# Layer 2's spectra: two frequency rows in one PSUM tile, copied together, the mirrored operand in its own order

## The chip, the cores and the metric

The kernel runs on one core of a Trainium2 chip. The metric is device time in microseconds of one execution; lower is better. All data are fp32. The engines are named as in the profile: PE (TensorE matmul; PEld is its weight load), DVE (VectorE), ACT (ScalarE), POOL (GpSimd), SP (SyncE, which here issues the DMAs).

## The reference, cut to what matters

Four layers, each adding to a residual `x` of shape (2, 128, 64, 64) what it makes of the group-normalised `x`. The change is in layer 2 alone: a 2-d real Fourier transform of the four quaternion parts (32 channels each), a product with complex weights of its own at each frequency, mixed over input channels by the quaternion rule, and the inverse transform.

```python
xs = jnp.stack([x[:, :q], x[:, q:2 * q], x[:, 2 * q:3 * q], x[:, 3 * q:]])
Xs = jnp.fft.rfft2(xs, s=(64, 64), axes=(-2, -1))
Ws = jnp.stack([kr_w + 1j * ki_w, kr_x + 1j * ki_x, kr_y + 1j * ki_y, kr_z + 1j * ki_z])
C = jnp.einsum('piohw,qbihw->pqbohw', Ws, Xs)
Pw = C[0, 0] - C[1, 1] - C[2, 2] - C[3, 3]
Px = C[0, 1] + C[1, 0] + C[2, 3] - C[3, 2]
Py = C[0, 2] - C[1, 3] + C[2, 0] + C[3, 1]
Pz = C[0, 3] + C[1, 2] - C[2, 1] + C[3, 0]
o = jnp.fft.irfft2(jnp.stack([Pw, Px, Py, Pz]), s=(64, 64), axes=(-2, -1))
```

There are 64 x 33 frequencies. Of the 64 rows over h, row m and row 64 - m (its mirror) come from the same real data.

## The kernel before, in words

Layers 0, 1 and 3 come before and after; layer 2 (`_layer2`) has three parts. First, the input is normalised, transposed and transformed over h into `y`, which stays in SBUF (lines 833 to 891). Last, the result is transformed back over h and added to `X` (from line 1117). Between them stands the part that the change touches: the transform over w, the products and the inverse over w, in eight blocks (`BLOCKS2`) of four frequency rows with their four mirrored rows.

One block `kb` goes like this. For a row m, `transposed` makes two transposes (L912, one per batch element) into a PSUM bank, copied by ACT to `yt` (L918). `transformed` multiplies `yt` with a constant (L925) and leaves in a PSUM bank `pe` (tag `pe`, two buffers of one bank) for each of the 128 channels the spectrum of the row and of its mirror: per batch element 2 images x 34 frequencies x (real, imaginary), 272 numbers in all. `placed` copies this into the operand `e` of the products: for each of the four output parts r, each quaternion part p is taken from channel group r xor p, with a sign. That is 12 copies per row and image of 136 elements per partition: one over 128 partitions with a sign per partition (`signs`), one over 64 and ten over 32. Image 0 is the row, image 1 the mirror, and each image has its own tile `e`, (128, 4 rows, 34, 16). Two rows go together through `rows_in`: `together` takes a step of each row's `placed` in turn, the copies of the first row all on ACT (L948) and those of the second all on DVE (L950).

`products` walks 17 pairs of frequencies (`PAIRS`) for the four rows of an image. Each pair is four products of `e` (32 columns) with the weights (L1008; in the profile each fp32 matmul is two instructions, so eight per group), in four column groups of the PE, whose results land in PSUM banks; DVE transposes them to `z` after each fourth pair (L1017), and L1025 adds and subtracts the parts into `pz`. A row of the mirrored image is stored so that row s of `e` meets row s of the weights, that is, in flipped order (`3 - row`). `turned` transposes `pz` (L1037) and ACT copies it to `pzt` (L1044); `back` transforms over w (L1062) and ACT copies into `y` (L1065).

The order is written out by hand, and each engine keeps it (`_in_order`). For each block, `alongside` runs the 17 groups of the direct products, and then the 17 of the mirrored ones, and after each group takes as many steps of the side generators as `n` says: beside the direct products the first two rows of the next block (`rows_in`, 8 of the steps in `n`) and the last block's `turned` and `back` (6); beside the mirrored ones the next two rows (8) and this block's `turned` (4). What is left of the sides when the products end runs after them. `rows_of_weights` (L823) loads the weights of one half-block on SP's queue, two DMAs of 2112 KB, into one of two buffers (`l2_w`, bufs=2), so a load is issued when the products of the half-block two before have ended. [...]

Of the kernel before, what the change touches and what calls it, by code (L numbers as in the profile page):

```python
# [10 lines left out]
F32 = mybir.dt.float32  # L11
# [5 lines left out]
B, C, H, W = 2, 128, 64, 64  # L17
S = H * W
CH = 512
# [81 lines left out]
def _load_consts(nc, pool, src, n):  # L101
    array, where = _CONSTS[n]
    t = pool.tile([128, array.shape[1]], F32, tag=f"consts{n}", name=f"consts{n}")
    nc.sync.dma_start(t, src)
    return {k: t[:rows, lo:hi] for k, (rows, lo, hi) in where.items()}
# [667 lines left out]
PAIRS = (FW + 1) // 2  # L773
# [29 lines left out]
def _layer2(ctx, tc, X, weights, cst, src, here=None, there=None, beside=None):  # L803


    nc = tc.nc
# [6 lines left out]
    k = _load_consts(nc, one, src, 1)  # L813
# [5 lines left out]
    def rows_of_weights(kb, mirror):  # L819

        ws = wpool.tile([128, 2, 32, NF], F32, tag="w", name="w_ri")
        for n, part in enumerate("ri"):
            nc.sync.dma_start(ws[:, n], weights[kb, mirror, part])  # L823
        return ws
# [5 lines left out]
    with tc.tile_pool(name="l2_a", bufs=3) as ap, tc.tile_pool(  # L830
        name="l2_aps", bufs=4, space=PSUM
# [17 lines left out]
        for b in range(B):  # L849
# [29 lines left out]
            def transformed(i, gt):  # L879
                py = aps.tile([128, CH], F32, tag="py", name="ps_py")  # L880
                for n in range(4):
                    cols = slice(n * 128, (n + 1) * 128)
                    nc.tensor.matmul(py[:, cols], gt[:, cols], k["fwd_h"], start=True, stop=True)
                nc.scalar.copy(
                    y[:, b, 8 * i : 8 * i + 8, :, :].rearrange("p w c f -> p (w c f)"), py
                )
# [11 lines left out]
    with tc.tile_pool(name="l2_e", bufs=4) as ep, tc.tile_pool(  # L898
        name="l2_ps", bufs=2, space=PSUM
    ) as psp, tc.tile_pool(name="l2_pz", bufs=1, space=PSUM) as pzp:  # L900

        def bank(tag="bank"):
            return psp.tile([128, CH], F32, tag=tag, name=f"ps_{tag}")

        def spectra(kb):

            return [(4 * kb + 1 + j) % (FH - 1) for j in range(4)]
# [10 lines left out]
            nc.scalar.copy(yt.rearrange("p b i -> p (b i)"), pt[:, : B * 128])  # L918
            return yt

        def transformed(m, yt):

            pe = bank("pe")
            for b in range(B):
                nc.tensor.matmul(  # L925
                    pe[:, b * 8 * PAIRS : (b + 1) * 8 * PAIRS],
                    yt[:, b, :],
                    k["fwd_w_both" if m else "fwd_w_ends"],
                    start=True,
                    stop=True,  # L930
                )
            return pe[:, : B * 8 * PAIRS].rearrange("p (b s f c) -> p b s f c", b=B, s=2, c=2)

        def placed(kb, m, got, image, e, scalar):

            row = (m - 1) % 4
            s, row = (1, 3 - row) if image else (0, row)

            def copied(r, p, n=1):
                to = slice(32 * p, 32 * p + 32 * n)
                of = slice(32 * (r ^ p), 32 * (r ^ p) + 32 * n)
                sign = signs if n == 4 else float(SIGN2[r][p])
                out = e[to, row, :, 4 * r : 4 * r + 4].rearrange("p f (b c) -> p b f c", c=2)
                sign = sign[to, :] if n == 4 else sign
                if scalar:
                    nc.scalar.mul(out, got[of, :, s], sign)  # L948
                else:
                    nc.vector.tensor_scalar_mul(out, got[of, :, s], sign)  # L950

            copied(0, 0, 4)
            copied(2, 2, 2)
            copied(2, 0)
            copied(2, 1)
            yield
            for r in (1, 3):
                for p in range(4):
                    copied(r, p)
                yield  # L960

        def together(*gens):

            gens = list(gens)
            while gens:
                for g in list(gens):
                    if next(g, gens) is gens:
                        gens.remove(g)
                yield

        def rows_in(kb, rows, places, es):

            yts = [transposed(m) for m in rows]
            yield
            gots = [transformed(m, yt) for m, yt in zip(rows, yts)]
            yield
            yield from copies(kb, rows, gots, places, es)

        def copies(kb, rows, gots, places, es):
            for image in places:  # L980
                if es[image] is None:
                    es[image] = ep.tile([128, 4, 2 * PAIRS, 8 * B], F32, tag="e", name="e")
                yield from together(
                    *(
                        placed(kb, m, got, image, es[image], i % 2 == 0)
                        for i, (m, got) in enumerate(zip(rows, gots))
                    )
                )

        def products(ws, e, pz):  # L990

            z = two.tile([128, PAIRS, 2, 4, 16], F32, name="z", bufs=1)
            zf = z.rearrange("p j n a x -> p (j n a x)")
            for j in range(PAIRS):
                last = j == PAIRS - 1
                if j % 4 == 0:
                    ph = bank() if last else pzp.tile([128, CH], F32, tag=f"z{j}", name="ps_z")  # L1000
                for s in range(4):
                    fw = s * FW + 2 * j
                    if last:
                        w = ws[:, :, :, fw : fw + 1].to_broadcast([128, 2, 32, 2])
                    else:
                        w = ws[:, :, :, fw : fw + 2]
                    out = ph[32 * s : 32 * s + 32, j % 4 * 128 : j % 4 * 128 + 128]
                    nc.tensor.matmul(  # L1008
                        out.rearrange("p (n f o) -> p n f o", n=2, f=2),
                        e[:, s, 2 * j : 2 * j + 2, :].rearrange("p f x -> p (f x)"),  # L1010
                        w.rearrange("p n o f -> p n f o"),
                        start=True,
                        stop=True,
                    )
                if j % 4 == 3 or last:
                    lo, n = j // 4 * CH, (j % 4 + 1) * 128
                    nc.vector.transpose(zf[:, lo : lo + n], ph[:, :n])  # L1017
                yield

            for c in range(2):  # L1020
                parts = [
                    z[:, :, n, 0::3, (c + n) % 2 :: 2]
                    for n in range(2)
                ]
                nc.vector.tensor_tensor(  # L1025
                    pz[:, :, :, c].rearrange("p x (j f) -> p j f x", f=2),
                    *parts,
                    ALU.add if c else ALU.subtract,
                )
            yield  # L1030
# [40 lines left out]
        def chain(*gens):  # L1071
            for g in gens:
                yield from g

        def alongside(main, side, steps):

            done = 0
            for n, _ in enumerate(main):
                while done < steps * (n + 1) / PAIRS:
                    next(side, None)  # L1080
                    done += 1
            for _ in side:
                pass

        pzs = [
            two.tile([128, 4 * B, 2 * PAIRS, 2], F32, name=f"pz{n}", bufs=1) for n in range(2)
        ]
        es = [None, None]
        first = spectra(0)
        for i in (0, 2):  # L1090
            for _ in rows_in(0, first[i : i + 2], (0,), es):
                pass
        before, later = None, []
        for kb in range(BLOCKS2):
            direct, image = [], []
            e, es = es, [None, None]
            nxt = spectra(kb + 1) if kb + 1 < BLOCKS2 else []
            side, n = [], 0
            if nxt:
                side.append(rows_in(kb + 1, nxt[:2], (1, 0), es))  # L1100
                n += 8
            if before:
                side += [turned(pzs[1], before[1]), back(kb - 1, *before)]
                n += 6
            else:
                later = side
                side, n = [rows_in(0, first[i : i + 2], (1,), e) for i in (0, 2)], 10
            alongside(products(rows_of_weights(kb, False), e[0], pzs[0]), chain(*side), n)
            side, n = [turned(pzs[0], direct)], 4
            if nxt:  # L1110
                side = later + [rows_in(kb + 1, nxt[2:], (1, 0), es)] + side
                n += 8 + 8 * len(later)
                later = []
            alongside(products(rows_of_weights(kb, True), e[1], pzs[1]), chain(*side), n)
            before = (direct, image)
        for _ in chain(turned(pzs[1], before[1]), back(BLOCKS2 - 1, *before)):
            pass
# [4 lines left out]
    with tc.tile_pool(name="l2_c", bufs=3) as cp, tc.tile_pool(  # L1122
        name="l2_cps", bufs=4, space=PSUM
# [1338 lines left out]
```

## Time and profile before

| | us |
|---|---|
| three runs | 4132.41, 4122.99, 4132.37 |
| median | 4132.37 |
| the profiled execution | 4122.99 |
| its span on the core | 4121.1 |

| stretch of the span, us | what | PE busy | DVE busy | ACT busy | mean granted PE clock | DMA share |
|---|---|---|---|---|---|---|
| 1918 to 2186 | layer 2, frequency blocks | 234.75 | 182.33 | 152.90 | 0.90 | 0.58 |
| 2186 to 2240 | layer 2 back over h, start of layer 3 | 41.90 | 28.84 | 19.14 | 0.82 | 0.18 |
| 2240 to 4121 | layer 3 | 1853.68 | 1398.69 | 1777.49 | 0.99 | 0.12 |

| line | what, in 1918 to 2186 | count | mean ns |
|---|---|---|---|
| L948 | ACT copy to `e`, 136 elements; with `signs` | 352; 32 | 282; 378 |
| L950 | DVE copy to `e`, 136 elements; with `signs` | 352; 32 | 297; 342 |
| L918 | ACT copy of 256 elements to `yt` | 36 | 373 |
| L1017 | DVE transpose of 512 elements to `z` | 64 | 712 |
| L925 | PE transform over w, 136 columns | 144 | 357 |
| L1008 | PE products, 128 columns | 2176 | 409 |

Matmuls are pipelined: the mean of one is its latency, and how fast they follow one another is read from the start times of the groups in the timeline. The timeline merges neighbouring instructions of one line into one row with a count. "Idle before" names what the engine waited for last.

### The profile page before, as it was taken

What the parts mean: (1) busy time and instruction counts of PE and PEld (TensorE: products, weight loads), DVE (VectorE), ACT (ScalarE), POOL (GpSimd) and SP (SyncE); (2) the same over time, 40 slices, a digit from 0 to 9 for tenths busy, and PEclk for the clock granted to TensorE, in tenths of its full rate; (3) what the DMA queues carried; (4) which work ended last, traced back from release to release, by engine and by line L of the source; (5) the groups of instructions that cost most, each with busy time, mean ns of one, the idle gap of its engine ahead of it and who ended that gap; (6) DMA issues with size and microseconds to landing.
All of it is one profiled execution on the core that took longest, in us unless ns stands there. A gap on an engine that the chain in (4) does not pass through costs nothing. (4 is left out here: it accounts for less than half of the span.)

```text
span 4121.1 us, 83188 instructions
## 1 busy us (share of the span) xinstructions
PE 3944.4 (96%) x35790; PEld 1382.1 (34%) x35790; DVE 3183.8 (77%) x3526; ACT 3228.6 (78%) x3907; POOL 72.2 (2%) x145
## 2 busy tenths in 40 slices
PE   7999999989999998997898999999999999999998
PEld 4522222245222223445665332223222332222222
DVE  4689999747989998986775878767777777766666
ACT  4478888734888884334654899999999999999998
POOL 1001000000000001000000000000000000000000
PEclk9999999999999999998998999999999999999999
DMA  1199970000000000003673211111112011110000
GB/s 49 24 192 180 181 104 2 2 2 2 2 2 2 1 2 13 0 1 132 254 281 104 74 32 34 43 43 32 32 34 67 19 32 32 36 53 6 6 6 4
DMA packets 193133, 217.66 MB, mean 53 GB/s; under 512 B 30441, under 2 KB 154345, under 8 KB 188658
## 3 DMA queue, kind: packets, MB, share of 16 engines
q1 hardware_dynamic: 192754, 212.25, 20.2%
q8 instruction: 282, 4.62, 0.5%
q14 instruction: 97, 0.79, 0.1%
HBM read 178.64 MB, written 98.57 MB: 67 GB/s over the span
## 5 line engine op out<-in xcount | busy, mean ns | idle before, releaser
L2181 ACT ACTIVATE weights<-ps_s 128x1024 f32<-128x1024 f32 x1920 | 1780.6, 1078 | 93.8 <-PE ps_s L2167 93.7
L1379 ACT ACTIVATE weights<-ps_s 128x1024 f32<-128x1024 f32 x1024 | 992.9, 1023 | 169.3 <-PE ps_s L1370 151.1
L2190 PE MATMUL ps_acc<-weights,vt 128*32 128x512 f32 x8192 | 1094.5, 606 | 0.0
L1827 DVE TENSOR_TENSOR sums<-sums,weights 128x2048 f32<-128x2048 f32 x384 | 880.0, 2292 | 43.7 <-ACT weights L1379 7.4
L2167 PE MATMUL ps_s<-q,k 64*128 64x512 f32 x4096 | 838.4, 472 | 6.3 <-DVE exp_i L2123 3.0
L2167 PEld LDWEIGHTS ps_s<-q,k 64*128 64x128 f32 x4096 | 352.7, 184 | 948.4 <-ACT weights L2181 824.7
L1370 PE MATMUL ps_s<-q,k 32*64 32x512 f32 x8192 | 631.5, 614 | 3.7 <-ACT weights L1379 1.5
L1787 PE MATMUL ps_acc<-weights,vt 128*32 128x512 f32 x4096 | 550.0, 605 | 7.2 <-ACT used L1817 3.7
L2139 DVE SCALAR_TENSOR_TENSOR exp_z<-exp_z,exp_m 128x1024 f32<-128x1024 f32 x384 | 469.7, 1223 | 11.2
L2123 DVE TENSOR_SCALAR exp_i<-ps_s 128x1024 int32<-128x1024 f32 x128 | 156.7, 1224 | 254.0 <-PE ps_s L2167 253.1
L1370 PEld LDWEIGHTS ps_s<-q,k 32*64 32x64 f32 x8192 | 162.0, 130 | 435.1 <-PE ps_s L1370 337.9
L2190 PEld LDWEIGHTS ps_acc<-weights,vt 128*32 128x32 f32 x8192 | 161.9, 108 | 304.2 <-issue 303.4
L1787 PEld LDWEIGHTS ps_acc<-weights,vt 128*32 128x32 f32 x4096 | 81.1, 108 | 426.6 <-issue 403.1
L662 DVE SCALAR_TENSOR_TENSOR X<-g,w,X 128x2048 f32<-128x2048 f32 x84 | 197.4, 2351 | 2.6
L1827 DVE TENSOR_TENSOR sums<-weights 128x2048 f32<-128x2048 f32 x64 | 146.6, 2291 | 62.8 <-ACT weights L1379 62.6
L2143 DVE SCALAR_TENSOR_TENSOR weights<-exp_z,exp_i 128x1024 f32<-128x1024 f32 x128 | 156.7, 1224 | 13.9
L1575 PE MATMUL ps_sp<-pad,diag 32*32 32x512 f32 x4608 | 159.8, 600 | 2.3 <-ACT q L1595 1.3
L2139 DVE SCALAR_TENSOR_TENSOR exp_z<-exp_m 128x1024 f32<-128x1024 f32 x128 | 155.9, 1218 | 0.0
L1008 PE MATMUL ps_z<-w_ri,e 128*32 128x128 f32 x2048 | 137.4, 409 | 14.5 <-DVE e L950 12.4
L1575 PEld LDWEIGHTS ps_sp<-pad,diag 32*32 32x32 f32 x4608 | 95.3, 103 | 55.5 <-issue 17.1
L950 DVE TENSOR_SCALAR e<-ps_pe 32x136 f32<-32x136 f32 (+1 forms) x352 | 104.4, 297 | 5.0
L2213 DVE STREAM_TRANSPOSE z<-ps_acc 128x512 f32<-128x512 f32 x32 | 22.9, 717 | 104.1 <-PE ps_acc L2190 104.1
(296 smaller groups left out, 2886.8 us busy)
## 6 DMA issues: line engine op xcount, KB each, us to landing
w_ri<-w_r SPq DMA_DIRECT2D x16, 2112.0 KB, 8.1
w_ri<-w_i SPq DMA_DIRECT2D x16, 2112.0 KB, 13.6
stack<-qs SPq DMA_DIRECT2D x64, 256.0 KB, 2.0
q<-stack SPq DMA_DIRECT2D x128, 128.0 KB, 2.5
k<-stack SPq DMA_DIRECT2D x128, 128.0 KB, 2.6
stack<-ks SPq DMA_DIRECT2D x32, 256.0 KB, 2.2
w_r<-in_L_conv_kr_w SPq DMA_DIRECT2D x15, 528.0 KB, 13.1
w_r<-in_L_conv_kr_x SPq DMA_DIRECT2D x15, 528.0 KB, 12.9
```

Of the source, the lines that this page charges most:

```text
L662: nc.vector.scalar_tensor_tensor(xi, g[:, i : i + H // 2, j : j + W], w8[:, s : s + 1], xi, ALU.mult, ALU.add)
L1370: nc.tensor.matmul(ps[j // 2][to, j % 2, :], k[rows, kt * 128 + 64 * half : kt * 128 + 64 * half + 64], q[rows, qb * CH : (qb + 1) * CH], ...
L1379: nc.scalar.activation(w[:, 2 * p : 2 * p + 2, :], ps[p], AF.Exp)
L1575: nc.tensor.matmul(ps[r // 2][to, r % 2, :].rearrange("p (h w) -> p h w", w=W), diag[rows, grp, t, :], pad[rows, y0 : y0 + ROWS, t % 3 : t ...
L1787: nc.tensor.matmul(ac[n][rows, :], lhs(rows), w[:, j, :], start=first, stop=last)
L1827: nc.vector.tensor_add(parts[0].rearrange("p j c -> p (j c)"), t.rearrange("p j c -> p (j c)"), w.rearrange("p j c -> p (j c)"),)
L2123: nc.vector.tensor_scalar(i, ps.rearrange("p j c -> p (j c)"), EXP_SCALE, EXP_BIAS, ALU.mult, ALU.add)
L2139: nc.vector.scalar_tensor_tensor(z, x, n, m, ALU.add, ALU.mult)
L2143: nc.vector.scalar_tensor_tensor(w.rearrange("p j c -> p (j c)"), z, EXP_TERMS[-1], power, ALU.add, ALU.mult)
L2167: nc.tensor.matmul(ps[j // 2][:, j % 2, :], g.k[kt // 4][rows, j // 2, keys], g.q[qb][rows, j // 2, :], start=True, stop=True,)
L2181: nc.scalar.activation(w[0], ps[p], AF.Exp)
L2190: nc.tensor.matmul(g.ac[32 * j : 32 * j + 32, :], g.vt[:, kt, j // 2, i : i + 2, :].rearrange("p a d -> p (a d)"), w[:, i, :], start=(at = ...
```

## The change

Two rows of a pair share one PSUM tile of two banks, `pe` of shape (128, 2, 512), with one buffer. Within a row the spectrum is laid out as (image, frequency, batch element, real or imaginary), so that the last two run together as the 4 columns that a copy writes to `e`; each matmul of L925 therefore writes runs of two elements with a step of four. One copy takes both rows, 272 elements per partition, and copies go to ACT and DVE in turn, counted by `turn`. The mirrored image is stored in the order of its rows, and `products` takes row `3 - s` of it. `together` and `copies` go.

```diff
-        def transformed(m, yt):
-
-            pe = bank("pe")
+        def transformed(m, yt, pe):
             for b in range(B):
                 nc.tensor.matmul(
-                    pe[:, b * 8 * PAIRS : (b + 1) * 8 * PAIRS],
+                    pe[:, :, b],
                     yt[:, b, :],
-                    k["fwd_w_both" if m else "fwd_w_ends"],
+                    k["fwd_w_both" if m else "fwd_w_ends"].rearrange("p (x c) -> p x c", c=2),
...
-        def placed(kb, m, got, image, e, scalar):
+        turn = [0]
+        def placed(m, got, image, e):
             row = (m - 1) % 4
-            s, row = (1, 3 - row) if image else (0, row)
...
-                out = e[to, row, :, 4 * r : 4 * r + 4].rearrange("p f (b c) -> p b f c", c=2)
+                out = e[to, row : row + 2, :, 4 * r : 4 * r + 4]
                 sign = sign[to, :] if n == 4 else sign
-                if scalar:
-                    nc.scalar.mul(out, got[of, :, s], sign)
+                turn[0] += 1
+                if turn[0] % 2:
+                    nc.scalar.mul(out, got[of, :, image], sign)
                 else:
-                    nc.vector.tensor_scalar_mul(out, got[of, :, s], sign)
+                    nc.vector.tensor_scalar_mul(out, got[of, :, image], sign)
...
         def rows_in(kb, rows, places, es):
             yts = [transposed(m) for m in rows]
             yield
-            gots = [transformed(m, yt) for m, yt in zip(rows, yts)]
+            pe = psp.tile([128, 2, CH], F32, tag="pe", name="ps_pe", bufs=1)
+            pairs = pe[:, :, : B * 8 * PAIRS].rearrange("p m (sf b c) -> p m sf b c", b=B, c=2)
+            got = pe[:, :, : B * 8 * PAIRS].rearrange("p m (s f x) -> p m s f x", s=2, x=2 * B)
+            for n, (m, yt) in enumerate(zip(rows, yts)):
+                transformed(m, yt, pairs[:, n])
             yield
-            yield from copies(kb, rows, gots, places, es)
-
-        def copies(kb, rows, gots, places, es):
             for image in places:
                 if es[image] is None:
                     es[image] = ep.tile([128, 4, 2 * PAIRS, 8 * B], F32, tag="e", name="e")
-                yield from together(
-                    *(
-                        placed(kb, m, got, image, es[image], i % 2 == 0)
-                        for i, (m, got) in enumerate(zip(rows, gots))
-                    )
-                )
+                yield from placed(rows[0], got, image, es[image])
...
-        def products(ws, e, pz):
+        def products(ws, e, image, pz):
...
-                        e[:, s, 2 * j : 2 * j + 2, :].rearrange("p f x -> p (f x)"),
+                        e[:, 3 - s if image else s, 2 * j : 2 * j + 2, :].rearrange("p f x -> p (f x)"),
```

## The prediction

> **What bounds the kernel now.** I read the page first. The chain of waits is no help here: it runs back only through layer 3 and names no line of layer 2. The costliest groups place the lines of the change: L948 and L950 (the signed copies) and L1008 (the products) have their first and last start between 1922 and 2183 us, so the frequency part of layer 2 is the stretch 1918 to 2186, 268 us of a span of 4121.1. Outside it nothing changes, so the question is how long this stretch takes. I then read the waits of that stretch, the timeline of one undisturbed block, and tables of short windows for the DMA and the clock.
>
> Waits of 1918 to 2186, columns: engine and line that waited, releaser, us in total, times, longest.
>
> ```profile
> PEld ps_z L1008 <- DVE e L950: 16.7, 9, 4.9
> PE ps_z L1008 <- DVE e L950: 12.4, 9, 4.4
> PEld ps_pe L925 <- ACT yt L918: 11.2, 16, 3.3
> PEld ps_bank L1062 <- ACT y L1065: 6.0, 6, 1.0
> ```
>
> PE is in order and has 235 of 268 us busy; what it waits for is above all the signed copies. Timeline of block kb=3, columns: start, length, engine, line, operation, idle before and its releaser.
>
> ```profile
> 2034.60 0.63 PE L1008 MATMUL ps_z<-w_ri,e 128*32 128x128 f32 x6
> 2036.13 0.62 PE L1008 MATMUL ps_z<-w_ri,e 128*32 128x128 f32 x2 [0.90 <-DVE e L950]
> 2036.69 0.88 PE L912 MATMUL ps_bank<-consts,y 128*128 128x128 f32 x4
> ...
> 2047.00 0.66 PE L1008 MATMUL ps_bank<-w_ri,e 128*32 128x128 f32 x8
> 2047.59 2.05 PE L1062 MATMUL ps_bank<-consts,pzt 66*128 66x128 f32 x16
> 2047.72 0.32 SPq L823 DMA_DIRECT2D w_ri<-w_r  x1
> 2048.09 0.43 SPq L823 DMA_DIRECT2D w_ri<-w_i  x1
> 2050.45 2.05 PE L1062 MATMUL ps_bank<-consts,pzt 66*128 66x128 f32 x16 [0.81 <-ACT y L1065]
> 2052.43 0.64 PE L1008 MATMUL ps_z<-w_ri,e 128*32 128x128 f32 x8
> ```
>
> The direct products of this block (F) run from 2034.60 to the group at 2047.00; the two inverse transforms of `back` (L1062) come after them, and only at 2052.43 do the mirrored products (T) begin, which end at 2063.75, where the next F starts. F's start loses time to the last copy of a row (L950), the second L1062 waits 0.81 us. The two SP lines are the next load of weights: it is issued when F's last product frees its buffer, and is needed at 2063.75. The load's landing (last column, us from its issue), one-microsecond windows (last two columns: DMA share, GB/s) and two windows with the granted clock (the column before those):
>
> ```profile
> w_ri<-w_i SPq DMA_DIRECT2D x1, 2112.0 KB, 13.6
> ...
> 2058.00:2059.00 1.00, 1.00 1.06 447
> 2059.00:2060.00 1.00, 1.00 0.42 177
> 2060.00:2061.00 1.00, 1.00 0.14 50
> ...
> 1971.30:1978.10 6.80, 3.94 (x50) 0.50 0.99 425
> 2080.30:2087.20 6.90, 5.22 (x50) 0.52 1.01 429
> ```
>
> A load saturates the DMA engines and has just ended when T ends; 13.6 us after the second issue is 2061.7, 2.05 us before it was needed. After a stretch in which PE idled much (1970.26 to 1972.54, waiting for `e`, or the wait between the two L1062) the clock is halved for some 7 us.
>
> **What the Trainium skill says.** "ScalarE: Activation LUTs", section "What ACT_TABLE_LOAD costs": 0.833 ns an element and about 93 ns for each pointer operand. The trace agrees: 372 ns for 256 elements and 585 for 512 is 0.832 each, and the copies with `signs` take 378 against 282 (96 ns). "VectorE: DVE Perf Modes", section "Why PSUM operands drop a tier": fp32 from PSUM goes at the basic rate; the trace has 295 ns for 136 elements and 692 for 512, 1.056 each. "Advanced Engine Details and Errata", section "PSUM Cachelines": non-contiguous patterns slow matmuls, and two consecutive elements should be contiguous for best throughput; no matmul of this trace writes broken runs, so nothing here shows it. "TensorE: Matmul & The Clock Gate", Part 1: after an idle window of about 3.4 us the clock is halved, and comes back after a busy one; the trace agrees (stretches of 3 to 10 us at 0.50).
>
> **The change part by part.**
>
> *Copies.* Now a pair of rows and one image costs ACT 378 + 11 x 282 = 3480 ns and DVE 342 + 11 x 297 = 3609 ns, one row each. After it is 12 copies of 272 elements in turn, the one with `signs` always on ACT. ACT: 378 + 113 = 491, 282 + 113 = 395, so 491 + 5 x 395 = 2466. DVE: 297 + 136 x 1.056 = 441, six times 2646. That saves 1.01 and 0.96 us per pair and image, 32 of them: 32 us on ACT, 31 on DVE. These engines don't bound the stretch (153 and 182 us busy of 268), so only PE's waits count. In a steady block the copies lie beside PE's products; if that cover were gone, these microseconds would count in full.
>
> *Order.* `together` gave four yields per image, the fourth empty; `placed` alone gives three. So `rows_in` is 8 steps instead of 10, which is what `alongside` was told. F has 14 steps: before, the sides had 16, and both `back` steps were left for after the products (2047.59 to 2052.43). Now they come after the 15th and 16th of the 17 groups. T has 12: the second `turned` no longer hangs over. The copies of T's second pair end two steps earlier, after group 10.
>
> *F after, at full clock.* From 17.83 us (2034.60 to 2052.43). The wait for `e` goes: 2034.60 to L912 is 2.08 us, where such a group before another kind takes 0.57 (2037.50 to 2038.07), so -1.5. What was late next on DVE are transposes of z, which nobody needs yet. The wait of the second L1062 for `y` goes, a product group lying between: -0.8. Two more changes of kind: +0.1. F = 15.6.
>
> *T after.* Same matmuls, 11.3 us. But the load it covers: from the start of F's last group (2047.00) to landing (2061.7) are 14.7 us, and T's first group now follows 0.45 us after that group. So the next F can begin 14.2 us after T did: PE waits 14.2 - 11.3 = 2.9 us. Before, the 4.85 us of L1062 stood between and hid it. The load for T has F's 15.6 us and stays hidden. What waits behind PE's first product of F is all of F, the transposes of the next pair too.
>
> So a steady block is 15.6 + 14.2 = 29.8 us, where the two blocks without a halved clock (kb 3 and 6) take 29.15. Blocks 1 to 6 take 1969.63 to 2155.78 = 186.2 us now, with five halved stretches that cost about 2.2 us each (31.5 against 29.15). After: 6 x 29.8 = 178.8, 0.5 for a rest of the wait in block 1, and halved stretches that fall into F (those in T hide behind the load). A gap of 2.9 us at F's start leaves a window of 3.4 us mostly idle in about half its positions: three times 2.2 = 6.6. Sum 185.9: nothing gained, bounds -7 (no stretch) and +7 (one in each).
>
> *Beginning.* Here copies are on the path. First pair to last copy: two pairs of copies, -1.0 each, and the second yt behind them; F of block 0 starts at 1929.4 instead of 1931.9: -2.5. T of block 0 waits 4.36 us for `e` at 1949.73; after, the last copies are issued after group 16 and lag by about 1.1: -3.2. Inside this T the second L925 comes 12.4 us after T's start (PE waited 1.68 for yt and 0.98 for `e`); after, the first pair's two images take DVE 5.3 + 0.7 from about 3.3, so L925 starts at 9.4, and the rest, with three more groups behind it, ends at 17.0 instead of 19.9: -2.9. The wait before F of block 7 (2155.78): -1.5. One halved stretch less in this part: -1.
>
> *Single tile `pe` with bufs=1.* Same two banks; L925 waits for both engines' copies of the former pair, which before it did bank by bank. In steady blocks they end half a stage earlier: 0. In block 0 it is in the 9.4 above.
>
> *Matmul output in runs of two.* L925 writes 68 runs of 2 elements, 16 bytes apart. Nothing in the trace prices it. Two elements stay together, so I take 0; from below 0, since fewer elements can't be written; from above three times the present 0.125 us per instruction (8 in 1.0 us): 2.0 us per pair.
>
> *Mirrored operand unflipped, `3 - s`.* An index at build time, the same 128x32 stationary operand: 0.
>
> Sum: -2.5 - 3.2 - 2.9 - 1.5 - 1 + 0 = -11 us. The profiled run took 4122.99 (span 4121.1 and 1.9 around it), so 4112 for such a run. The median of three is 4132.37, two of them at 4132.4; the change doesn't touch what lies between them, so 4132.4 - 11 = 4121.
>
> **The rivals.** (A) As above: the load becomes the bound of T and takes back what the copies give. For it: a landing only 2.05 us early behind a cushion of 4.85. 4121, own range 4114 to 4128. (B) The loads don't bind: since F now overlaps the next issue with a load in flight, its start (about 3 us from issue to full rate) is hidden, and the 2.9 us per block aren't paid: -11 - 6 x 2.9 = -28, 4104. Against it: F's load is issued when none is in flight, the one before having landed after 14.2 of 15.6 us. (C) The gaps halve the clock in each F: three more stretches, -11 + 7 = -4, 4128. (D) The broken PSUM runs: at 2.0 us per pair, T's seven pairs hide in the load's 2.9, the other 11 don't: -11 + 22 = +11, 4143. It decides from half that price (1.0 us per pair); for it is the general sentence of the skill, against it that pairs stay contiguous.
>
> **How the numbers follow.** A measurement here tells about 0.3% (12.4 us) from no change. A 0.60, of it 0.24 beyond -12.4 and 0.36 within; B 0.12, faster; C 0.14, within; D 0.14, of it 0.09 slower by more, 0.05 within. Rounded with a little for the spread of runs: faster 0.36, same 0.54, slower 0.10. The range leaves out the far end of D and of B: 4104 to 4138.
>
> **What would show it.** Right: PE's wait at the first L1008 of each F put down to the DMA of w_ri, 2 to 3 us, six or seven times; L1062 before the last group; `e` waits gone from steady blocks; copies of 272 at 395 and 441 ns; the DMA share of the stretch up. Wrong: F starting without a wait (B), L925 over 0.2 us per instruction (D), or copies above 500 ns, which would bring the `e` waits back.

## The result, and the profile after

The changed kernel takes 4196.61 us (median; 4192.24 to 4201.7), the kernel before 4129.9 us beside it: a ratio of 1.0164, 95% interval [1.0151, 1.0178]. The profiled execution took 4194.96 us with a span of 4193.1, 72 us more than that of before. All of it is in the stretch of the frequency rows: the last inverse transform starts at 2258.58 instead of 2186.65 us, 71.9 us later, and what follows takes as long as before.

The waits of that stretch, now 1918 to 2260, columns as before (engine and line that waited, releaser, us in total, times, longest). The lines have moved: L947 is ACT's signed copy, L949 DVE's, L994 the products, L1023 the transposes of `turned`, L1030 the copy into `pzt`, L1048 the inverse transforms, L924 the forward transform.

```profile
DVE e L949 <- ACT e L947: 115.2, 163, 4.7
ACT e L947 <- DVE e L949: 97.7, 174, 1.8
...
PE ps_bank L994 <- ACT pzt L1030: 28.8, 7, 6.3
PE ps_bank L1048 <- ACT pzt L1030: 25.9, 7, 4.3
...
PE ps_pe L924 <- DVE e L949: 14.3, 3, 7.3
```

The first two lines did not exist before: DVE's copies wait for ACT's and ACT's for DVE's, 337 times. A copy needs nothing that the other engine's copy makes. They are handed from one engine to the other all the same, and PE waits for `pzt` ahead of the last group of T and ahead of the inverse transforms in F, seven times each. In the kernel before, each engine read a tile of its own, and both copied at once. Here, in F of kb=3, three copies of DVE lie inside the 3.24 us of eleven copies of ACT:

```profile
2039.23 3.24 ACT L948 ACTIVATE e<-ps_pe 64x136 f32<-64x136 f32 x11
...
2039.75 0.92 DVE L950 TENSOR_SCALAR e<-ps_pe 64x136 f32<-64x136 f32 x3
```

The timeline of a steady block of the changed kernel (F of kb=4) shows how the one leads to the other:

```profile
2108.65 2.18 PE L924 MATMUL ps_pe<-consts,yt 128*128 128x136 f32 x8
...
2110.86 0.49 ACT L947 ACTIVATE e<-ps_pe,signs 128x272 f32<-128x272 f32 x1 [2.33 <-PE ps_pe L924]
2111.39 0.43 DVE L949 TENSOR_SCALAR e<-ps_pe 64x272 f32<-64x272 f32 x1 [2.89 <-ACT e L947]
2111.86 0.39 ACT L947 ACTIVATE e<-ps_pe 32x272 f32<-32x272 f32 x1 [0.50 <-DVE e L949]
2112.28 0.44 DVE L949 TENSOR_SCALAR e<-ps_pe 32x272 f32<-32x272 f32 x1 [0.46 <-ACT e L947]
...
2121.53 0.39 ACT L947 ACTIVATE e<-ps_pe 32x272 f32<-32x272 f32 x1 [0.50 <-DVE e L949]
2121.95 1.06 ACT L1030 COPY pzt<-ps_bank 66x512 f32<-66x512 f32 x2
2121.95 0.43 DVE L949 TENSOR_SCALAR e<-ps_pe 32x272 f32<-32x272 f32 x1 [0.45 <-ACT e L947]
...
2122.58 3.78 PE L1048 MATMUL ps_bank<-consts,pzt 66*128 66x128 f32 x16 [4.27 <-ACT pzt L1030]
2126.88 3.78 PE L1048 MATMUL ps_bank<-consts,pzt 66*128 66x128 f32 x16
```

Read the start of each copy against the end of the one above it: 2110.86 + 0.49 is 2111.35, and DVE starts at 2111.39; its copy ends at 2111.82, and ACT starts at 2111.86. At no time do two of these copies run at once. The 24 copies of the pair take 2110.86 to 2122.38, 11.5 us, where two engines side by side would take 5.3 by the prediction's prices (2 x 2646 ns). Each copy is as short as it was costed (0.39, 0.49, 0.44). In the program's order the copy into `pzt` stands behind ACT's last signed copy, so it comes only at 2121.95, though its input was ready by about 2117.3 (the transposes of `turned` at 2116.65 took 0.63). The inverse transforms need `pzt`: PE stands still for 4.27 us. Then its clock is halved (0.50 granted from 2122.58 to 2126.30), and each group of 16 takes 3.78 us instead of the 2.05 of before.

The T before it (of kb=3) shows the same wait, there ahead of its last group of products, whose PSUM bank is held until `pzt` has been copied out:

```profile
2105.31 1.07 ACT L1030 COPY pzt<-ps_bank 66x512 f32<-66x512 f32 x2
...
2105.95 0.66 PE L994 MATMUL ps_bank<-w_ri,e 128*32 128x128 f32 x8 [3.75 <-ACT pzt L1030]
```

Most of the stretch, up to 2240, in the table of windows (columns: window, its length, busy us of PE, weight loads, DVE, ACT and POOL, granted clock, DMA share, GB/s):

```profile
1918.00:2240.00 322.00, 241.86 (x2549) 166.34 (x2548) 145.70 (x294) 116.11 (x270) 0.00 (x0) 0.76 0.48 187
```

ACT and DVE are less busy than in the kernel before (116 and 146 us, before 153 and 182 in the whole stretch), and the stretch is longer. The granted clock is 0.76, before 0.90.

A steady block adds up. From the issue of weights at the end of one F to that at the end of the next (2090.43 to 2131.32, so T of kb=3 and F of kb=4) it takes 40.9 us. PE's work at full clock, as the prediction has it, is 15.6 + 11.3 = 26.9. The two waits for `pzt` are 4.27 + 3.75 = 8.0. The halved clock is 2 x 1.73 on L1048, 0.99 and 0.70 on the two L924 (2.18 and 1.89 for 1.19), 2 x 0.41 on the two L912 (1.12 for 0.71): 6.0. Sum 40.9.

### The profile page after: what moved, and what is told of

Read it like the earlier page. It is cut to its first block, busy times and chain, and to the rows that moved or that the text cites. A ratio compares the mean times of both kernels' runs of the same rounds, so it can differ in the third digit from the quotient of the medians.

```text
span 4193.1 us, 82793 instructions
## 1 busy us (share of the span) xinstructions
PE 3966.2 (95%) x35790; PEld 1398.4 (33%) x35790; DVE 3153.4 (75%) x3334; ACT 3195.6 (76%) x3715; POOL 74.4 (2%) x145
## 5 line engine op out<-in xcount | busy, mean ns | idle before, releaser
L949 DVE TENSOR_SCALAR e<-ps_pe 32x272 f32<-32x272 f32 (+1 forms) x192 | 83.8, 437 | 116.1 <-ACT e L947 115.2
L2129 DVE SCALAR_TENSOR_TENSOR weights<-exp_z,exp_i 128x1024 f32<-128x1024 f32 x128 | 156.6, 1224 | 14.7 <-ACT weights L2167 1.0
L994 PE MATMUL ps_z<-w_ri,e 128*32 128x128 f32 x2048 | 135.0, 408 | 8.7 <-DVE e L949 8.7
L947 ACT ACTIVATE e<-ps_pe 32x272 f32<-32x272 f32 x160 | 62.4, 390 | 90.7 <-DVE e L949 90.7
```

The source lines that it names most:

```text
L2129: nc.vector.scalar_tensor_tensor(w.rearrange("p j c -> p (j c)"), z, EXP_TERMS[-1], power, ALU.add, ALU.mult)
```

## The experiments

In all of them a "block" is the mean of six, from the issue of weights at the end of T of block 0 to that at the end of T of block 6. It is 31.4 us in the kernel before and 40.8 in the changed one.

Two theories. By tile: two engines that read one PSUM tile are put in order, whichever banks and partitions they read. By bank: only reads of the same bank are, so two engines on two banks run side by side. A third, that the copies of 272 with their output across two rows are slow or need the order themselves, is tried on the way.

**rows_apart.** The tile of two banks stays; copies are again of 136, row 0 (first bank) on ACT, row 1 (second bank) on DVE.

```
-                out = e[to, row : row + 2, :, 4 * r : 4 * r + 4]
-                (in turn: ACT or DVE copies got[of, :, image])
+                nc.scalar.mul(e[to, row, :, 4 * r : 4 * r + 4], got[of, 0, image], sign)
+                nc.vector.tensor_scalar_mul(e[to, row + 1, :, 4 * r : 4 * r + 4], got[of, 1, image], sign)
```

> The tile of two banks stays, but each copy takes one row of 136 elements: the first row's on ACT out of the first bank, the second row's on DVE out of the second. Theory T (two engines that read one PSUM tile are put in turn by a wait, whatever the banks): 48 copies of a pair stand in one chain of about 0.33 us each, some 16 us where the changed kernel has 24 of 0.445, so slower than the changed kernel: about 4265 us. Rival K (the turn comes from both engines touching one bank): no waits between copies, near the kernel before with the new order of steps, 4105 to 4140. Rival S (the broken output runs of the transform, or the doubled copies, cost the time): 4130 to 4150, since copies are single again.

4268.1 us, ratio 1.0346 [1.0321, 1.0371]; a block takes 49.6 us. The engines read different banks and still take turns, now 48 copies to a pair:

```profile
2103.00 0.28 ACT L944 ACTIVATE e<-ps_pe 64x136 f32<-64x136 f32 x1 [0.43 <-DVE e L945]
2103.31 0.29 DVE L945 TENSOR_SCALAR e<-ps_pe 64x136 f32<-64x136 f32 x1 [0.34 <-ACT e L944]
```

The instructions, and which engine reads which row, are those of the kernel before, where they ran side by side from two tiles of one bank each. By bank falls.

**image_one_tile and image_two_tiles.** The spectra are sorted by image instead of by row: the row image lies in one bank and the mirror image in the other. DVE copies the row image, ACT the mirror image (where only one image is copied, in block 0, the engine goes by pair), copies of 272. For this the forward transform is cut into two matmuls of 68 columns. The two kernels differ only in the tile: one of two banks, or two of one bank each.

```
 image_one_tile   pe = psp.tile([128, 2, CH], F32, tag="pe", name="ps_pe", bufs=1)
 image_two_tiles  pes = [psp.tile([128, CH], F32, tag=f"pe{s}", name="ps_pe", bufs=1) for s in range(2)]
 both             for s in range(2):
                      nc.tensor.matmul(pe[...s...][:, :, b], yt[:, b, :], over[:, s], start=True, stop=True)
```

> One tile of two banks, but sorted by image: the mirror of both rows in the one bank, copied by ACT, the rows in the other, copied by DVE, 272 elements each, four copies of one engine and four of the other in turn. The transform over w is cut in two of 68 columns. Theory T: still one chain, with six handovers per pair instead of 24, so near the changed kernel: 4175 to 4195 us. Rival K (by bank): like the run with two tiles, 4110 to 4130.

> As the run with one tile sorted by image, with a tile of its own for each bank, and nothing else. Theory T: no waits between ACT and DVE; the prediction's sum then holds, with the load of weights as the bound of the mirrored half: 4119 us (4110 to 4130), with PE waiting 2 to 3 us for the DMA at the start of each direct half. If the load doesn't bind: about 4104. Rival S (copies of 272 or the broken runs are dear in themselves): 4180 or more.

One tile: 4188.73 us, 1.015 [1.0131, 1.0169]. Two tiles: 4134.16 us, 1.002 [1.0011, 1.0029]. The banks, the copies and the matmuls are the same, and the declaration of the tile is worth 54.6 us. The timeline with one tile, where the engines change after every four copies:

```profile
2095.06 1.34 DVE L943 TENSOR_SCALAR e<-ps_pe 64x272 f32<-64x272 f32 x3
2096.43 1.59 ACT L941 ACTIVATE e<-ps_pe 32x272 f32<-32x272 f32 x4 [1.93 <-DVE e L943]
...
2098.06 1.79 DVE L943 TENSOR_SCALAR e<-ps_pe 32x272 f32<-32x272 f32 x4 [1.66 <-ACT e L941]
```

ACT begins at 2096.43, where the last of DVE's copies ends (2095.06 + 1.34 = 2096.40), and DVE goes on at 2098.06, after ACT's 1.59 us (2098.02). With two tiles no wait of a copy for the other engine is left, and PE's waits for `pzt` shrink to 0.2 us. So neither the place of the data nor the banks that the engines read set the order. The profile infers from semaphore events what released an instruction, so these waits stand in the program as it was built; no run here shows the chip itself holding back a copy.

What PE waits for with two tiles at the start of F is the load:

```profile
PE ps_z L998 <- DMA w_ri<-w_i: 5.9, 3, 2.9
```

The range for two tiles was missed by 4 us. Forward transforms cut in two cost more than was allowed for: a pair takes 1.97 to 2.0 us at full clock (16 matmuls of 68 columns), where 8 of 136 take 1.16 to 1.19. The second pair in the beginning also waits 5.0 us for a bank that now only one engine empties. That these two make up the 4 us was not tried.

**engine_by_pair.** The changed kernel with one line of it changed: all copies of the first pair on DVE, all of the second on ACT.

```
-                turn[0] += 1
-                if turn[0] % 2:
+                if row == 2:
                     nc.scalar.mul(out, got[of, :, image], sign)
```

> The changed kernel with one line different: all copies of a block's first pair of rows on DVE, all of its second on ACT. Tile, banks, copies of 272, strided output and order of steps stay. Theory T: no waits between the engines; DVE has 10.6 us of copies and 4.3 of transposes and sums in the direct half of 15.6, ACT 9.7 of copies in the mirrored half: 4115 to 4140 us. Rivals that blame the tile's single buffer, the double copies or the strided output: 4180 or more.

4138.91 us, 1.0029 [1.0018, 1.004]. The tile of two banks, the copies of 272, the output across two rows, the broken runs of the matmul and the new order are all still there; only the alternation is gone, and with it 57.7 of the 66.7 us. So none of those carries the loss of the steady blocks, which take 31.2 us (before 31.4). The beginning stays as late as in the changed kernel: the load at the end of T of block 0 is issued at 1983.54 us (1984.56 there, 1966.89 before), for with one engine to a pair its copies follow one another in any case. In the blocks there remains that ACT copies the whole second pair, 24 copies or 9.6 us at 490 and 390 ns each, ahead of `pzt`:

```profile
PE ps_bank L992 <- ACT pzt L1028: 20.8, 7, 5.4
```

**order_alone.** The kernel before with only the new order of steps.

```
                     if next(g, gens) is gens:
                         gens.remove(g)
-                yield
+                if gens:
+                    yield
```

> The kernel before with only the new order of steps (three steps per image instead of four); one-bank tiles, copies of 136 elements and the flipped store as before. This tests the prediction's step on the order by itself: F should have both inverse transforms ahead of its last group, so F about 16 to 17.5 us (the waits for e stay, 1 to 1.5 us), and T should be followed by a wait of PE for the DMA of w_ri, about 2 to 3 us, since the cushion of 4.85 us is gone. Theory that the load binds T: steady block 30 to 31.5 us, total within 10 us of before (4118 to 4135). Rival, the loads do not bind: steady block 28 us, 4105. Rival, the new order itself carries part of the loss of after: over 4145.

4118.51 us, 0.9988 [0.9979, 0.9997]; a block takes 30.4 us. In the timeline both inverse transforms (L1063) stand ahead of F's last group, T follows at once, and F of the next block (2087.66) waits for the load:

```profile
2068.40 2.05 PE L1063 MATMUL ps_bank<-consts,pzt 66*128 66x128 f32 x16
...
2070.95 2.05 PE L1063 MATMUL ps_bank<-consts,pzt 66*128 66x128 f32 x16
2072.93 0.64 PE L1009 MATMUL ps_bank<-w_ri,e 128*32 128x128 f32 x8
2073.38 0.66 PE L1009 MATMUL ps_z<-w_ri,e 128*32 128x128 f32 x8
...
2087.66 0.64 PE L1009 MATMUL ps_z<-w_ri,e 128*32 128x128 f32 x8 [2.90 <-DMA w_ri<-w_i]
```

From T's first product to F's are 14.28 us; the prediction had 14.2, and 2.9 for the wait. Each F from block 2 to block 7 starts after such a wait, of 2.8 to 3.4 us. The profile names the DMA for two of the six, and for the others work on `z` or `pz` by DVE; all six start 13.9 to 14.5 us after the issue of the load (2073.64 to 2087.66 here), so it is most likely the load each time.

**copies_from_sbuf.** The changed kernel with one copy more: ACT takes the tile of two banks to SBUF in one instruction, and the signed copies, in turn on ACT and DVE as in the change, read it there.

```
+            flat = two.tile([128, 2, used], F32, name="flat")
+            nc.scalar.copy(flat, pe[:, :, :used])
-            got = pe[:, :, : B * 8 * PAIRS].rearrange("p m (s f x) -> p m s f x", s=2, x=2 * B)
+            got = flat.rearrange("p m (s f x) -> p m s f x", s=2, x=2 * B)
```

> The changed kernel with one more step: ACT copies the two-bank tile once into SBUF (544 elements, estimate 544 x 0.832 + 113 = 566 ns), and the signed copies of 272, in turn on ACT and DVE as in the change, read it there. Theory that the loss comes from two engines reading one PSUM tile, which puts the copies in a chain: no copy waits for the other engine any more, 12 copies of an image take about 2.5 us, T is bounded by the load as predicted, steady block 29.8 to 30.5 us, total 4110 to 4128. Rival, the copies of 272 with their interleaved output or the shared destination tile e cause the chain: the copies still hand over, total 4190 or more (after plus 18 evictions).

4117.04 us, 0.9981 [0.9973, 0.999]; a block takes 30.1 us. Two engines read one tile here too, and write one `e`, in turn, and none waits for the other:

```profile
2092.30 0.53 ACT L947 ACTIVATE e<-flat,signs 128x272 f32<-128x272 f32 x1
2092.31 0.60 DVE L949 TENSOR_SCALAR e<-flat 64x272 f32<-64x272 f32 x2 [5.88 <-ACT flat L971]
2092.84 2.20 ACT L947 ACTIVATE e<-flat 32x272 f32<-32x272 f32 x5
...
2093.69 1.83 DVE L949 TENSOR_SCALAR e<-flat 32x272 f32<-32x272 f32 x6
```

Between 2092.30 and 2095.52 ACT makes six copies and begins a seventh, and DVE makes eight. The order is a matter of PSUM tiles, and not of the tile `e` or of the shape of the copies. The copy of 544 elements took 614 ns for the 566 expected: the 113 ns in that sum are the price of 136 elements (136 x 0.832), while the fixed part of such a copy is the rest of its 282 ns, 169. The costs from SBUF, in the groups by shape (count, busy us, mean ns):

```profile
L947 ACT ACTIVATE e<-flat 32x272 f32<-32x272 f32 x160 | 68.8, 430 | 1.9
L949 DVE TENSOR_SCALAR e<-flat 32x272 f32<-32x272 f32 x160 | 47.0, 294 | 2.3
L971 ACT COPY flat<-ps_pe 128x544 f32<-128x544 f32 x18 | 11.1, 614 | 28.2 <-PE ps_pe L924 28.2
```

**copies_from_sbuf_balanced and order_balanced.** Both with the second inverse transform of `back` moved from F into T, so that PE has about 13.5 us of work in each half beside a load of 13.6.

```
-                side += [turned(pzs[1], before[1]), back(kb - 1, *before)]
-                n += 6
+                last = back(kb - 1, *before)
+                side += [turned(pzs[1], before[1]), one_step(last)]
+                n += 5
...
+            if before:
+                side = side[:-1] + [last] + side[-1:]
+                n += 1
```

> copies_from_sbuf, and the second of the two inverse transforms of back goes from F into T, so that both halves of a block take PE about 13.5 us (15.6 + 11.3 = 26.9, halved) beside a load of 13.6 us. If the load is what bounds T in copies_from_sbuf (2 to 3 us of wait at each F), this takes most of it back: block 28 to 28.6 us, some 8 to 12 us under copies_from_sbuf, 4100 to 4115. If the load does not bind, no difference (within 4 us).

> order_alone with the same move of the second inverse transform from F into T. If the load binds order_alone, 5 to 12 us under it (4108 to 4125); copies in rows of 136 keep the waits for e of 1 to 1.5 us a half, so it should not beat copies_from_sbuf_balanced. If copies bind, no difference from order_alone.

4099.81 us, 0.9945 [0.9927, 0.9963], and 4101.59 us, 0.9952 [0.9934, 0.997]: both about half a percent faster than the kernel before, 17 us under their pairs without the move, and not to be told from each other, though the one makes half as many signed copies as the other. A block takes 27.7 and 28.5 us. Waits of PE for the load remain, but short ones, in this list of copies_from_sbuf_balanced up to 2170:

```profile
PE ps_z L997 <- DMA w_ri<-w_i: 7.0, 8, 1.7
```

The move gave more than expected (17 us for 8 to 12, and for 5 to 12). The clock is a likely part of the rest: over 1969.6 to 2155 it is granted in full. Why is not shown. The waits are shorter, but that doesn't settle it: before, the clock was halved after waits of 0.8 us too (the second L1062 at 1988.12, which took 3.57 us).

```profile
1969.60:2155.00 185.40, 177.02 (x2297) 114.11 (x2290) 99.43 (x237) 104.15 (x219) 0.00 (x0) 1.00 0.76 301
```

## Why the prediction was wrong

It forecast 4121 us, and 4196.6 came, with the sign reversed. The step that failed is the paragraph *Single tile `pe` with bufs=1*: "Same two banks; L925 waits for both engines' copies of the former pair, which before it did bank by bank. In steady blocks they end half a stage earlier: 0." It asked what the single tile does to its next writer and not what it does to its two readers. The first sentence of *Copies* rests on the same gap: it counts ACT's 2466 ns and DVE's 2646 ns beside each other. Their durations were right, but it is their sum that a pair of rows and one image takes: 5.1 us, and 5.8 with the handovers and with transposes to `z` that DVE does in between (half of 11.5). The place at which to see it was named by the Trainium skill: "PSUM — Partial Sum Buffer", section "PSUM bank collisions raise a hardware error", says that accesses of two engines to one bank and the same 32 partitions must not coincide, reads of ScalarE and VectorE included, and that the program has to keep them apart. The kernel before obeyed that with a bank to each engine and row; the change gave both engines both banks. The runs are stricter than the page: copies in different banks (rows_apart, image_one_tile) were ordered as well, as long as the tile was one, and so were copies in different quarters of the partitions (the copies at 2111.86 and 2112.28 above read partitions 64 to 95 and 96 to 127). None of the rivals held this, D included.

Point by point:

- *Copies.* 490, 390 and 437 ns for the forecast 491, 395 and 441. Half the instructions, right durations. But with the new order of steps in place even copies that do run side by side bring nothing that can be seen: copies_from_sbuf (4117.04, with 18 copies to SBUF more) and order_alone (4118.51, still 48 small copies to a pair) can't be told apart. They lay beside other work, as the prediction said of steady blocks.
- *Order.* Right: both L1048 follow the 15th and the 16th group of F, also in the changed kernel.
- *F after*, *T after.* Without the chain both hold. In order_alone and in copies_from_sbuf six F's wait, 2.6 to 3.5 us each; the trace names the DMA of `w_ri` for two of them in the one run and for three in the other. In the changed kernel T takes 16.2 us, longer than the load, so the DMA wait that the prediction looked for doesn't appear: its main sign failed for another reason than the one it gave (B). That the load binds once the chain is gone was shown by the move of one inverse transform, which took 17 us off.
- *Beginning.* F of block 0 was to start at 1929.4 us; its first full set of rows came at 1935.82. The second L924 waits 5.17 us for the single tile, whose 12 copies run one after another. Inside T of block 0 PE waits 7.27 us more for it: the second L924 starts 15.4 us after T (1954.99 to 1970.36), where the prediction had 9.4. F of block 1 starts at 1984.30 instead of 1969.63: +14.7 for a forecast -8.6. Blocks 1 to 6 then take 244.9 us instead of 186.2, +58.8 for a forecast 0. The end gives back 1.5. Sum 72.0, the difference of the profiled runs.
- *Clock.* The prediction had gaps of 2.9 us at the start of F halve the clock in three of six blocks, at 2.2 us each. In order_alone and copies_from_sbuf, which have these gaps, all six are followed by 0.79 in the next 8 us, so some 3.4 us of half clock; they catch little but the forward transform (in order_alone 2.18 us for 1.19), about 1 us each. That is twice as often and half as dear; that the 6.6 us forecast is about what they cost is luck. In the changed kernel waits of about 4 us, twice a block, bring a clock of 0.76 over 1918 to 2240. The Trainium skill has it that the clock is halved after an idle window of about 3.4 us ("TensorE: Matmul & The Clock Gate", Part 1); here waits of 2.6 us were enough each time, and in the kernel before some of 0.8 us. The 6.0 us a block is read from durations in the trace; no run held the clock and kept the waits.
- *Matmul output in runs of two.* Right at 0, and rival D with it: at full clock 8 of them take 1.17 to 1.19 us, before 1.16 to 1.19. (The 1.0 us for 8 in the prediction is too low: from 2038.07 to 2039.19, the starts of such a group and of the next, are 1.12.) That fits the Trainium skill, "Advanced Engine Details and Errata", section "PSUM Cachelines", in that each two elements stay together; the general slowing of broken patterns that it states doesn't show with runs of two.
- *`3 - s`.* Stayed in engine_by_pair and copies_from_sbuf with no cost visible.

With the chain taken out and nothing else undone, copies_from_sbuf has a ratio of 0.9981 where the prediction's -11 us on 4132.4 is 0.9973: 4121 was a fair forecast of a change whose copies could run side by side, though in part by luck. Up to F of block 1, from there to F of block 7 and behind it the prediction had -9.6, 0 and -1.5 us (its 1 us of clock is in the first); the profiled copies_from_sbuf has -4.4, -2.5 and -3.1, and order_alone, with the copies of before, -6.4, -0.6 and -3.0. Both come to -10.0, so no part of the gain can be put down to the halved copies.

Open is what the ordering would cost if it went by bank and quarter of the partitions (32 each), as the page states it: two engines reading one PSUM tile without the wait was not tried.

## What to carry to other kernels

When a change puts two buffers into one, list everything that touches the new one, readers too, and ask of each pair of engines who will now wait for whom. In this program a PSUM tile read by two engines is a queue with one place, and alternating engines over it is worse than one engine for all copies of a pair (4196.6 against 4138.9 us). Where two engines shall share the work, give each its own tile, or take the data to SBUF once. And before cutting work that lies beside a transfer, find when the transfer lands: here fewer copies were worth nothing that can be told from the spread of runs, before PE's work was split evenly between the two loads (4117.0 and 4118.5 us) or after (4099.8 and 4101.6). The split, an edit of a few lines, brought 17 us.

## What the runs showed of the hardware

- A handover between ACT and DVE costs little by itself: from the end of one copy to the start of the next are about 0.04 us (2111.35 to 2111.39). The loss is the overlap, and what stands behind in ACT's queue.
- DVE copies 272 fp32 elements in 437 ns from PSUM and in 294 ns from SBUF. The difference, 143 ns, is half of 1.056 ns an element, which fits the Trainium skill, "VectorE: DVE Perf Modes", section "Why PSUM operands drop a tier" (a PSUM operand holds fp32 to the basic rate). ACT goes the other way, 390 ns from PSUM and 430 from SBUF.
- A forward transform of 136 columns cut into two of 68 costs 1.97 to 2.0 us instead of 1.16 to 1.19 for a pair of rows, at full clock.
